# Two float32r parts in place of three bfloat16 parts in the dense products of a two-layer graph network

## The chip, the cores and the metric

The kernel runs on one core of one Trainium2 chip. The metric is the device time of one execution in microseconds (us); the median of the runs shown is 3284.89 us. The engines are TensorE (PE, with its weight loads listed apart as PEld), VectorE (DVE), ScalarE (ACT), GpSimd (POOL) and the queue of SyncE (SP), which issues most of the DMAs.

## The reference, cut to what matters

`x` has 12,500 rows of 256 float32 values, and 200,000 edges lead from row `src` to row `dst`. The edges are sorted by `dst`, and `dst` is far denser at the low rows than at the high ones.

```python
def _sage_conv(x, src, dst, W_l, b_l, W_r):
    msgs = x[src]
    agg = jax.ops.segment_sum(msgs, dst, num_segments=N_NODES)
    deg = jax.ops.segment_sum(jnp.ones((src.shape[0],), x.dtype), dst, num_segments=N_NODES)
    mean = agg / jnp.maximum(deg, 1.0)[:, None]
    return mean @ W_l + b_l + x @ W_r
h = jax.nn.relu(_sage_conv(x, src, dst, W1_l, b1, W1_r))
h = jax.nn.relu(_sage_conv(h, src, dst, W2_l, b2, W2_r))
return h @ W3 + b3
# and around it: layernorm(x + the above)
```

All weights are 256 x 256. The costly part is the sum over the edges, which is made twice: once of rows of `x` and once of rows of `h`.

## The kernel before, in words

Rows are handled in `NB` = 98 blocks of 128, and the 256 columns in `NC` = 2 halves. `layer` (line 602) runs twice, once per layer, and in each layer two ways of summing run side by side.

**Gathered sums.** Edges of the sparse destinations are handled in rounds. A round is four indirect DMAs on POOL (`gathered`, L262), each fetching 128 rows of the table into one of four buffers `got`; then eight short fp32 matmuls on PE (L274) sum neighbouring rows into `part_ps`, ACT copies that to `some` (L284), two fp32 products (L290) spread it over 128 columns, and DVE adds it to a ring of sums (L304). Layer 1 has 269 rounds (1076 indirect DMAs), layer 2 has 235 (940). A buffer `got` can be filled again when the matmuls of the round four earlier are done.

**Dense products.** The densest destinations are handled in groups of `DN` = 256: five in layer 1 (0 to 4), eight in layer 2 (0 to 7). For a group, `count` (L724) makes on PE and DVE a table of how many edges lead from each row to each of the 256 destinations, evicted by ACT (L782) as bfloat16 to one of two buffers `counts`. `product` (L681) then multiplies the rows of the whole table by the counts. Counts are small whole numbers, exact in bfloat16; the float32 rows are made exact as a sum of three bfloat16 parts (`exact`, L656), stored to `x3_d` and `h3_d`. So a block of rows and a group take 3 parts x 2 halves = 6 matmuls of 256 columns (L707), whose stationary operand is a 128 x 128 piece of the rows and whose moving operand is the counts. In layer 2, which needs the same counts of groups 0 to 3 again, layer 1 has saved them to `count_d` (`stored`, L829), and the product of group 4 to 7 from the resident counts runs with that of group 0 to 3 from streamed counts beside it, on the same stationary operand: 12 matmuls a block, alternating between `dense_ps` and `beside_ps`.

Rows come by SP (L693), two blocks a DMA, 384 KB, into `NROWS` = 4 buffers, so eight blocks may be on the way or waiting. A load is made to wait for the gather matmuls that follow the product that read the same buffer four loads earlier (L701), because those matmuls signal anyway.

**Order.** PE and POOL run in the order in which the program emits instructions (`manual_schedule`, L459); the other engines' orders are made by the framework's scheduler. In `layer`, after each gather round the generator `dense` is advanced until its accumulated cost estimate reaches a share of the total that is proportional to the rounds done (`due`, L642), in three thirds with pieces of finished blocks between them. The estimates are constants: `COST_DENSE` 0.7 per block and group, `COST_SPLIT`, `COST_DEGREES`, and `count_cost`. `mixed` interleaves the parts of a stage. In layer 1 a stage is the product of group g-1 beside the count of group g, and the first stage splits `x` beside the count of group 0. Layer 2 has four stages, one per pair of groups, the middle two of them with a count beside.

Finished blocks of 128 destinations go through `first_block` or `last_block` (fp32 matmuls with the weights at L902, L925, L930, L997); `first_block` also stores the block's `h` and its parts.

## Time and profile before

| | |
|---|---|
| median of 3 runs | 3284.89 us (3281.76 to 3287.56) |
| the profiled execution | 3281.46 us, span 3279.7 us |
| mean granted TensorE clock | 0.888 of full speed |
| gather rounds | layer 1 from 11.5 to 1719 us, layer 2 from 1753 to 3234 us |
| DMA | 612.56 MB, mean 187 GB/s |

Busy time of an engine is the sum of its instructions' durations. Matmuls are pipelined, and a matmul's listed duration (282 ns for 256 columns) is longer than the distance from its start to the next one's (0.11 us), so PE's cost is read from distances between starts. "Idle before, releaser" after a group names what ended the waits of that group; "remote" or "another core or an unknown queue" is a semaphore for which the profile finds no sender at that moment. Lines named below are those of the kernel before.

### The profile page before, as it was taken

Reading aid. Unit: us, or ns where it says so; the run is one execution under the profiler, and the core shown is the slowest. Engines: PE = TensorE matmul, PEld = TensorE weight load, DVE = VectorE, ACT = ScalarE, POOL = GpSimd, SP = SyncE. Lnnn points to the kernel's source line nnn. Section 1 sums busy time; section 2 is a strip of 40 time slices with the busy share of each in tenths; the row PEclk is TensorE's granted clock in tenths of the full one; section 3 lists DMA queues with packets and bytes.
Section 4 is the critical chain, followed back from the end, with each engine's and each line's share of the span. In section 5 each row is a group of like instructions: output and inputs, shape, how many; then the busy total and the mean of one; then the engine's idle time right before and its main releaser. Section 6 shows DMA issues by size and latency. Waiting matters only on the chain.

```text
span 3279.7 us, 56146 instructions
## 1 busy us (share of the span) xinstructions
PE 2574.5 (79%) x18946; PEld 1733.1 (53%) x18946; DVE 1566.5 (48%) x5560; ACT 1151.6 (35%) x2331; POOL 1967.7 (60%) x2026
## 2 busy tenths in 40 slices
PE   4565668878878878889865887878889888888876
PEld 2122335545546656656643555556556666666654
DVE  6778675544445555555552122334345444343334
ACT  0423664444444444455441001223233333221122
POOL 6665666666665656666664666565666666556652
PEclk9766679979979989989987899989989999999998
DMA  5565668658658758647644566565556656566642
GB/s 123 164 185 171 179 205 274 209 159 262 209 156 289 225 174 266 221 144 238 222 142 122 181 183 184 176 181 166 177 167 192 184 170 183 164 200 198 204 139 84
DMA packets 375242, 612.56 MB, mean 187 GB/s; under 512 B 72111, under 2 KB 253989, under 8 KB 374949
## 3 DMA queue, kind: packets, MB, share of 16 engines
q1 hardware_dynamic: 273235, 343.33, 34.0%
q0 software_dynamic: 96768, 264.37, 26.7%
q8 instruction: 155, 2.54, 0.3%
q10 hardware_dynamic: 4946, 1.19, 0.2%
q14 instruction: 138, 1.13, 0.1%
HBM read 518.75 MB, written 89.92 MB: 186 GB/s over the span
## 4 chain that ended last, share of the span: by engine, by line
PE 59%; issue 8%; another core or an unknown queue 7%; DVE 5%; ACT 3%; DMA 3%; POOL 0%; ACTq 0%; DVEq 0%; SPq 0%; POOLq 0%
PE dense_ps L707 16%; PE part_ps L274 7%; PE count_ps L776 7%; PE beside_ps L707 6%; PE block_ps L925 6%; PE block_ps L930 5%; PE sum_ps L290 4%; PE block_ps L997 3%; PE block_ps L902 3%; DMA rows<-x_d 2%; ACT counts L782 2%; PE count_ps L780 1%; PE sum_ps L296 1%; PE dense_ps L797 1%
## 5 line engine op out<-in xcount | busy, mean ns | idle before, releaser
L262 POOL DMA_INDIRECT got<-in_x_dram,src_t x1076 | 1067.8, 992 | 649.6 <-issue 258.2
L262 POOL DMA_INDIRECT got<-h_d,src_t x940 | 897.7, 955 | 617.1 <-issue 230.8
L707 PE MATMUL dense_ps<-counts,rows 128*128 128x256 bf16 x5292 | 981.6, 282 | 58.9 <-issue 31.5
L707 PEld LDWEIGHTS <-rows 128*128 128x128 bf16 x7644 | 745.2, 101 | 327.6 <-issue 165.6
L782 ACT CAST counts<-count_ps 128x882 f32 (+3 forms) x688 | 611.3, 888 | 533.1 <-PE count_ps L776 135.6
L707 PE MATMUL beside_ps<-spare,rows 128*128 128x256 bf16 x2352 | 570.3, 282 | 24.2 <-issue 23.2
L776 PE MATMUL count_ps<-pick,low 128*128 128x490 bf16 (+2 forms) x1188 | 378.7, 371 | 145.0 <-ACT counts L782 64.3
L274 PE MATMUL part_ps<-got,one 128*32 128x257 f32 (+1 forms) x4032 | 385.4, 434 | 53.2 <-issue 21.7
L738 DVE TENSOR_SCALAR pick<-steps,key_t 128x686 bf16<-128x686 f16 (+3 forms) x816 | 332.6, 410 | 117.6 <-remote 32.1
L218 DVE TENSOR_TENSOR one<-lo_t,lane_b 128x128 f32<-128x128 bf16 x504 | 144.1, 286 | 470.7 <-remote 150.1
L284 ACT COPY some<-part_ps 128x257 f32<-128x257 f32 (+1 forms) x355 | 132.8, 374 | 643.4 <-remote 293.7
L741 DVE TENSOR_SCALAR low<-lanes,low_t 128x130 bf16<-128x130 f16 x816 | 221.0, 272 | 212.4 <-remote 72.5
L304 DVE TENSOR_TENSOR sums<-sums,sum_ps 128x256 f32 x355 | 145.6, 410 | 250.2 <-remote 110.6
L290 PE MATMUL sum_ps<-two,some 128*128 128x128 f32 x1420 | 241.1, 296 | 13.1 <-issue 8.3
L290 PEld LDWEIGHTS sum_ps<-two,some 128*128 128x128 f32 x1420 | 211.2, 207 | 32.2 <-issue 19.3
L776 PEld LDWEIGHTS <-low 128*128 128x128 bf16 x1188 | 121.1, 103 | 181.9 <-issue 62.7
L936 DVE TENSOR_TENSOR own<-block_ps,biases 128x256 f32<-128x256 f32 x196 | 82.4, 420 | 220.3 <-PE block_ps L930 106.5
L274 PEld LDWEIGHTS part_ps<-got,one 128*32 128x32 f32 x4032 | 89.1, 113 | 184.1 <-issue 161.1
L925 PE MATMUL block_ps<-w1l_sb,sums 128*128 128x256 f32 x352 | 123.5, 483 | 69.7 <-issue 31.5
L933 ACT COPY sums<-zero 128x256 f32<-128x256 f32 x170 | 68.7, 404 | 306.0 <-PE block_ps L930 142.6
L904 ACT COPY own_t<-block_ps 128x256 f32<-128x256 f32 x294 | 109.3, 375 | 183.4 <-remote 65.4
L746 DVE TENSOR_SCALAR aft<-steps,after_t 128x98 bf16<-128x98 f16 x689 | 173.6, 252 | 0.0
(184 smaller groups left out, 2678.7 us busy)
## 6 DMA issues: line engine op xcount, KB each, us to landing
rows<-x_d SPq DMA_DIRECT2D x245, 384.0 KB
rows<-h_d SPq DMA_DIRECT2D x196, 384.0 KB
count_d<-counts SPq DMA_DIRECT2D x28, 896.0 KB
spare<-count_d SPq DMA_DIRECT2D x196, 128.0 KB
x_sb<-in_x_dram SPq DMA_DIRECT2D x194, 128.0 KB
x_d<-split SPq DMA_DIRECT2D x98, 192.0 KB
h_d<-split SPq DMA_DIRECT2D x98, 192.0 KB
got<-in_x_dram,src_t POOLq DMA_INDIRECT x1076
```

The lines of the kernel that those rows point to most:

```text
L262: rows = nc.gpsimd.indirect_dma_start(out=g[:, j, :D], out_offset=None, in_=self.table, in_offset=bass.IndirectOffsetOnAxis(ap=src_t[:, e: ...
L274: strip = nc.tensor.matmul(part_ps[j * W:(j + 1) * W, :width], lhsT=one[:, j], rhs=g[:, j, :width], start=r == 0, stop=r == n - 1)
L290: nc.tensor.matmul(sum_ps[:, c], lhsT=some[:, c * P:(c + 1) * P], rhs=two, start=True, stop=True)
L304: nc.vector.tensor_add(own, own, sum_ps[:, :NC])
L707: nc.tensor.matmul(t[:, c], lhsT=rows[:, b % 2, k, c * P:(c + 1) * P], rhs=d, start=False, stop=b == NB - 1 and k == 2 and c == NC - 1)
L738: nc.vector.tensor_scalar(r[:, :w * NB], steps[:, :w * NB], key_t[g][:, t - lo_g:t - lo_g + 1], None, op0=OP.is_equal)
L741: nc.vector.tensor_scalar(low.rearrange("p (a b) -> p a b", a=5), lanes_5[:, :, :LW // 5], low_t[:, t:t + 1], None, op0=OP.is_equal)
L746: nc.vector.tensor_scalar(aft.rearrange("p (a b) -> p a b", a=7), steps_7[:, :, :NB // 7], after_t[g][:, t - after_from[g]:t - after_from[ ...
L776: nc.tensor.matmul(c[:, a * NB:b * NB], lhsT=s, rhs=r[:, a * NB:b * NB], start=True, stop=alone)
L782: nc.scalar.copy(to[:, :, bass.ds(off_act.at(t), w)], c.rearrange("p (d s) -> p s d", s=NB))
L925: product = nc.tensor.matmul(ps[:, 0], lhsT=agg[:, c], rhs=wl[:, c], start=c == 0, stop=c == NC - 1)
L930: product = nc.tensor.matmul(ps[:, 1], lhsT=own_t[:, c], rhs=wr[:, c], start=c == 0, stop=c == NC - 1)
```

## The change

The rows are split in two float32 parts instead of three bfloat16 parts: the upper part is the float32 value with its low 12 bits cleared by an integer AND, the lower part is the rest. Both have at most 12 significant bits. They are stored as float32 (2048 bytes a row instead of 1536) and multiplied in the type float32r; the counts, which stay bfloat16 in SBUF, are copied to float32 by ACT first (`widened`), into three buffers. Weight loads of float32r are part of the matmul instruction; those of bfloat16 are instructions of their own.

In layer 1 (`product`) a block and a group now take 2 x 2 = 4 matmuls of 256 columns. In layer 2 (`products`) two groups whose counts lie side by side are one moving operand of 512 columns: a block and a pair take 4 matmuls of 512 columns. The pairs are (4,5) resident, then (0,1) and (2,3) streamed while groups 6 and 7 are counted, then (6,7) resident. Rows are loaded one block a DMA (256 KB) into `NROWS` = 6 buffers. A streamed block of a pair's counts is one DMA of 1024 bytes a partition as before. `COST_DENSE` goes from 0.7 to 0.5 and `COST_SPLIT` from 0.8 to 0.7.

Small tables move: the key tables become views of one tensor whose space is used for streamed counts and `w3` in layer 2, offset lists lie in `spare` and in a new `lists`, one bias row and `w3` are loaded between the layers, and `low` has 5 buffers instead of 6. The products' leading matmul with zeros (L689) is left out in layer 2.

```diff
-    x3_d = dram.tile([P, NB, 3, D], BF16, name="x3_d")
-    h3_d = dram.tile([P, NB, 3, D], BF16, name="h3_d")
-    count_d = dram.tile([HG1 - 1, P, NB, DN], BF16, name="count_d")
+    x2_d = dram.tile([P, NB, 2, D], F32, name="x2_d")
+    h2_d = dram.tile([P, NB, 2, D], F32, name="h2_d")
+    SAVED = list(range(HG1 - 1)) + list(range(HG1 + 1, HG - 2))
+    count_d = dram.tile([P, NB, len(SAVED), DN], BF16, name="count_d")
...
-    NROWS = 4
+    NROWS = 6
...
             pieces()
 
-    def exact(t, s, rest):
-
-        def upper(a):
-            return a.bitcast(BF16).rearrange("p (n h) -> p n h", h=2)[:, :, 1]
-
-        leaves = nc.vector.tensor_tensor(rest, t, upper(t), op=OP.subtract)
-        nc.vector.tensor_tensor(s[:, 2], rest, upper(rest), op=OP.subtract)
-        nc.scalar.copy(s[:, 0], upper(t))
-        nc.scalar.copy(s[:, 1], upper(rest))
+    def exact(t, s):
+
+        leaves = nc.vector.tensor_scalar(s[:, 0].bitcast(I32), t.bitcast(I32), -4096, None,
+                                         op0=OP.bitwise_and)
+        nc.vector.tensor_tensor(s[:, 1], t, s[:, 0], op=OP.subtract)
         return leaves
 
     def split_rows(b):
         t = load_rows(x, N, b, "split_sb")
         s = split[:, b % 2]
-        leaves = exact(t, s, work.tile([P, D], F32, name="rest", tag="own"))
+        leaves = exact(t, s)
         if b < 3:
             later(leaves)
-        nc.sync.dma_start(x3_d[:, b], s)
-
-    STREAMS = 4
-    streams = [spare.bitcast(BF16)[:, i * 2 * DN:(i + 1) * 2 * DN].rearrange("p (b d) -> p b d", b=2)
-               for i in range(STREAMS)]
+        nc.sync.dma_start(x2_d[:, b], s)
+
+    STREAMS = 6
+    used_tables = tables[:, :sum(widths[:2 * HG1 + 2])]
+    flat = [(t.bitcast(BF16), n) for t, n in ((spare, 4), (used_tables, STREAMS - 4))]
+    streams = [t[:, i * 2 * DN:(i + 1) * 2 * DN].rearrange("p (g d) -> p g d", g=2)
+               for t, n in flat for i in range(n)]
     n_streamed = 0
 
-    def product(table3, g, c_sb, beside=None):
-
+    def loaded(table2, b, pair=None, ahead=0):
 
         nonlocal n_streamed
-        ps = [dense_pool.tile([P, NC, DN], F32, name="dense_ps")]
-        if beside is not None:
-            ps.append(beside_pool.tile([P, NC, DN], F32, name="beside_ps"))
-        for t in ps:
-            nc.tensor.matmul(t, lhsT=zeros_b, rhs=c_sb[:, :NC, :DN], start=True, stop=False)
+        rows = work.tile([P, 2, D], F32, name="rows", bufs=NROWS)
+        loads = [(nc.sync.dma_start(rows, table2[:, b]), NROWS)]
+        counted = both[:, b, :, :DN]
+        if pair is not None:
+            counted = streams[n_streamed % STREAMS]
+            n_streamed += 1
+            loads.append((nc.sync.dma_start(counted, count_d[:, b, pair:pair + 2]), STREAMS))
+
+        for load, n in loads:
+            n -= ahead
+            if len(used) >= n and used[-n] < len(strips):
+                tc.add_manual_dep(load.ins, strips[used[-n]], LANDED, reason="products done")
+        return rows, counted
+
+    WIDE = 3
+
+    def widened(counted):
+        wide = work.tile([P, 2, DN], F32, name="wide", bufs=WIDE)
+        nc.scalar.copy(wide.bitcast(F32R), counted)
+        return wide
+
+    def product(table2, g, c_sb):
+
+        ps = dense_pool.tile([P, NC, DN], F32, name="dense_ps")
+        nc.tensor.matmul(ps, lhsT=zeros_b, rhs=c_sb[:, :NC, :DN], start=True, stop=False)
+        wide = {}
         for b in range(NB):
-            if b % 2 == 0:
-                rows = work.tile([P, 2, 3, D], BF16, name="rows", bufs=NROWS)
-                loads = [(nc.sync.dma_start(rows, table3[:, b:b + 2]), NROWS)]
-                if beside is not None:
-                    stream = streams[n_streamed % STREAMS]
-                    n_streamed += 1
-                    loads.append((nc.sync.dma_start(stream, count_d[beside, :, b:b + 2]), STREAMS))
-
-                for load, n in loads:
-                    if len(used) >= n and used[-n] < len(strips):
-                        tc.add_manual_dep(load.ins, strips[used[-n]], LANDED, reason="products done")
-            counted = [c_sb[:, b, :DN]] + ([stream[:, b % 2]] if beside is not None else [])
-            n = 0
-            for k in range(3):
+            rows, _ = loaded(table2, b)
+            for u in range(b - b % 2, min(b + 2 * WIDE - 3, NB), 2):
+                if u not in wide:
+                    wide[u] = widened(c_sb[:, u:u + 2, :DN])
+            of = wide[b - b % 2]
+            for k in range(2):
                 for c in range(NC):
-                    for t, d in zip(ps, counted):
-                        nc.tensor.matmul(t[:, c], lhsT=rows[:, b % 2, k, c * P:(c + 1) * P], rhs=d,
-                                         start=False, stop=b == NB - 1 and k == 2 and c == NC - 1)
-                        n += 1
-                        if n == 3 * NC and beside is not None:
-                            yield COST_DENSE
-            if b % 2:
-                used.append(len(strips))
+                    nc.tensor.matmul(ps[:, c], lhsT=rows[:, k, c * P:(c + 1) * P].bitcast(F32R),
+                                     rhs=of[:, b % 2].bitcast(F32R), start=False,
+                                     stop=b == NB - 1 and k == 1 and c == NC - 1)
+            used.append(len(strips))
             yield COST_DENSE
         d_sb = work.tile([P, NC, DN], F32, name="d_sb", bufs=1)
-        nc.scalar.copy(d_sb, ps[0])
+        nc.scalar.copy(d_sb, ps)
         yield g, d_sb
-        if beside is not None:
-            b_sb = split.rearrange("p two k d -> p (two k d)").bitcast(F32)[:, :NC * DN].rearrange(
-                "p (c d) -> p c d", c=NC)
-            nc.scalar.copy(b_sb, ps[1])
-            yield beside, b_sb
+
+    def products(table2, g, pair):
+
+        ps = [pool.tile([P, 2, DN], F32, name=name)
+              for pool, name in ((dense_pool, "dense_ps"), (beside_pool, "beside_ps"))]
+        rows, wide = {}, {}
+        for b in range(NB):
+            for u in range(b, min(b + WIDE, NB)):
+                if u not in wide:
+                    rows[u] = loaded(table2, u, pair, u - b)
+                    wide[u] = widened(rows[u][1])
+            (own, _), of = rows.pop(b), wide.pop(b)
+            for k in range(2):
+                for c in range(NC):
+                    nc.tensor.matmul(ps[c], lhsT=own[:, k, c * P:(c + 1) * P].bitcast(F32R),
+                                     rhs=of.bitcast(F32R), start=b + k == 0,
+                                     stop=b == NB - 1 and k == 1)
+                if k == 0:
+                    yield COST_DENSE
+            used.append(len(strips))
+            yield COST_DENSE
+        d_sb = work.tile([P, NC, DN], F32, name="d_sb", bufs=1)
+        b_sb = split.rearrange("p two k d -> p (two k d)")[:, :NC * DN].rearrange("p (c d) -> p c d", c=NC)
+        for i, t in enumerate((d_sb, b_sb)):
+            for c in range(NC):
+                nc.scalar.copy(t[:, c], ps[c][:, i])
+            yield g + i, t
 
     def count(g, to):
 
...
         nc.vector.reciprocal(rdeg[:, n0:n0 + DN // P], deg)
 
-    COST_DENSE, COST_DEGREES, COST_SPLIT = 0.7, 1.6, 0.8
+    COST_DENSE, COST_DEGREES, COST_SPLIT = 0.5, 1.6, 0.7
 
     def count_cost(t):
         n = 1 if room(t) * NB <= 512 else 2
...
                 p[2] += cost
                 yield cost * scale
 
-    def stored(g, c_sb):
+    def stored(g):
         for b0 in range(0, NB, 14):
-            nc.sync.dma_start(count_d[g, :, b0:b0 + 14], c_sb[:, b0:b0 + 14, :DN])
+            nc.sync.dma_start(count_d[:, b0:b0 + 14, SAVED.index(g)], counts[g % 2][:, b0:b0 + 14, :DN])
             yield 0.5
 
-    def dense(table3, waiting, with_deg, g, c_sb, beside=None):
-        made = []
-        for p in product(table3, g, c_sb, beside):
+    def dense(waiting, made, with_deg=None):
+        ready = []
+        for p in made:
             if isinstance(p, float):
                 yield p
             else:
-                made.append(p)
-        if with_deg:
-            yield from degrees(g, c_sb)
-        for g, d_sb in made:
+                ready.append(p)
+        if with_deg is not None:
+            yield from degrees(with_deg, counts[with_deg % 2])
+        for g, d_sb in ready:
             for j in range(DN // P):
                 waiting.append((g * (DN // P) + j, d_sb[:, :, j * P:(j + 1) * P]))
 
...
     def stages_2(waiting):
 
-        for beside, g in enumerate(range(HG1 - 1, HG)):
-            parts = [(dense(h3_d, waiting, False, g, counts[g % 2], beside), D_2)]
-            if HG1 <= g < HG - 1:
-                parts.append((count(g + 1, counts[(g + 1) % 2]), counting(g + 1)))
-            yield parts
+        def passed(g):
+            pair = SAVED.index(g) if g in SAVED else None
+            return dense(waiting, products(h2_d, g, pair)), D_2
+
+        def next_counts(gs):
+            for g in gs:
+                yield from count(g, counts[g % 2])
+                if g in SAVED:
+                    yield from stored(g)
+
+        yield [passed(HG1 - 1)]
+        before = SAVED[:HG1 - 1:2]
+        for g in range(HG1 + 1, HG, 2):
+            saved = [passed(s) for s in before]
+            yield [(chain.from_iterable(p for p, _ in saved), sum(c for _, c in saved)),
+                   (next_counts((g, g + 1)),
+                    sum(counting(i) + (MOVED if i in SAVED else 0.0) for i in (g, g + 1)))]
+            before = [g]
+        yield [passed(HG - 2)]
 
...
         s = split[:, b % 2]
-        exact(h, s, own)
-        nc.sync.dma_start(h3_d[:, b], s)
+        exact(h, s)
+        nc.sync.dma_start(h2_d[:, b], s)
```

More of the change, by code (lines that the diff above doesn't have):

```diff
@@ L1 @@
 from contextlib import ExitStack
+from itertools import chain
 import concourse.bass as bass
@@ L8 @@
 F32 = mybir.dt.float32
+F32R = mybir.dt.float32r
 F16 = mybir.dt.float16
@@ L140, in by_runs @@
     lo2 = consts.tile([P, len(groups)], F32, name="lo2")
-    place = consts.tile([1, len(groups)], I32, name="place")
     low_t = consts.tile([P, HT], F32, name="low_t")
```

47 lines of the change are left out of this document (30 added, 17 removed).

## The prediction

> **What bounds the kernel now.** I read the page's busy times first, then the chain that ended last, then the costliest groups.
>
> ```profile
> PE 2574.5 (79%) x18946; PEld 1733.1 (53%) x18946; DVE 1566.5 (48%) x5560; ACT 1151.6 (35%) x2331; POOL 1967.7 (60%) x2026
> PE 59%; issue 8%; another core or an unknown queue 7%; DVE 5%; ACT 3%; DMA 3%; POOL 0%; ACTq 0%; DVEq 0%; SPq 0%; POOLq 0%
> L262 POOL DMA_INDIRECT got<-in_x_dram,src_t x1076 | 1067.8, 992 | 649.6 <-issue 258.2
> L707 PE MATMUL dense_ps<-counts,rows 128*128 128x256 bf16 x5292 | 981.6, 282 | 58.9 <-issue 31.5
> L707 PE MATMUL beside_ps<-spare,rows 128*128 128x256 bf16 x2352 | 570.3, 282 | 24.2 <-issue 23.2
> ```
>
> PE is the busiest and holds 59% of the chain, and the products that the change shortens (L707, 7644 matmuls) are its largest part. That alone would promise much. Their real price is in PE's timeline, from start to start:
>
> ```profile
> 2819.82 0.61 PE L290 MATMUL sum_ps<-two,some 128*128 128x128 f32 x4
> 2820.27 0.27 PE L707 MATMUL dense_ps<-counts,rows 128*128 128x256 bf16 x1
> 2820.38 0.27 PE L707 MATMUL beside_ps<-spare,rows 128*128 128x256 bf16 x1
> 2820.49 0.27 PE L707 MATMUL dense_ps<-counts,rows 128*128 128x256 bf16 x1
> ```
>
> A bfloat16 matmul of 256 columns takes 0.109 us. Four fp32 pieces of 128 columns, each with a weight load of its own, take 0.45, so 0.112 each.
>
> But whole stretches tell another story. The columns: us, then busy us and instructions of PE, PEld, DVE, ACT, POOL, then clock, DMA share, GB/s.
>
> ```profile
> 531.00:654.00 123.00, 101.32 (x787) 66.58 (x785) 65.67 (x276) 59.84 (x108) 77.84 (x81) 0.93 0.67 211
> 1817.00:1937.00 120.00, 98.48 (x718) 64.95 (x716) 21.85 (x67) 11.97 (x32) 76.52 (x81) 0.90 0.60 182
> 2955.00:3077.00 122.00, 107.23 (x850) 81.45 (x850) 42.91 (x133) 22.50 (x65) 75.98 (x81) 0.97 0.67 202
> 400.00:1700.00 1300.00, 1069.15 (x8480) 717.55 (x8480) 695.04 (x2679) 627.89 (x1181) 800.87 (x823) 0.89 0.68 212
> 1780.00:3150.00 1370.00, 1155.35 (x8727) 835.38 (x8728) 492.07 (x1587) 334.26 (x711) 833.28 (x873) 0.93 0.60 182
> ```
>
> In the first three, PE issues 718 to 850 matmuls, DVE works 22 to 66 us, ACT 12 to 60, and yet each has 81 gathers in 120 to 123 us: a round of four takes 5.9 to 6.1 us whatever PE does. POOL's timeline shows why:
>
> ```profile
> 2952.68 0.94 POOL L262 DMA_INDIRECT got<-h_d,src_t  x1 [0.30 <-issue]
> 2954.97 0.95 POOL L262 DMA_INDIRECT got<-h_d,src_t  x1 [1.35 <-remote]
> 2956.23 0.95 POOL L262 DMA_INDIRECT got<-h_d,src_t  x1 [0.31 <-issue]
> 2957.48 0.95 POOL L262 DMA_INDIRECT got<-h_d,src_t  x1 [0.30 <-issue]
> 2958.74 0.95 POOL L262 DMA_INDIRECT got<-h_d,src_t  x1 [0.30 <-issue]
> 2961.01 0.95 POOL L262 DMA_INDIRECT got<-h_d,src_t  x1 [1.32 <-PE sum_ps L290]
> ```
>
> Three gathers follow at 1.25 us; the first of a round, which waits for PE's matmuls on its buffer, comes 2.3 us after the one before. 3 x 1.25 + 2.3 = 6.05. The extra 1.04 us is hardly PE's work: PE's completion signals reach the other engines in bursts, and of 2,423 between 60 and 3200 us 678 arrive 1.9 to 2.2 us after the start of the last gather, a time that makes up 4% of that stretch. They come when POOL has just gone idle. Of 503 rounds, 58 start at once (5.0 to 5.2 us), some 270 take 6.0 to 6.4, some 124 over 6.6, and only these last are plainly PE's. Averaged over each layer's stretch (823 and 873 gathers above), a round takes 6.32 and 6.28 us, 0.27 and 0.23 over 6.05.
>
> **The change part by part.**
> *Products, layer 1.* 490 blocks and groups go from 6 x 0.109 to 4 matmuls of 256 columns. No float32r runs before the change, so I bound it: 0.109 (the bfloat16 row) to 0.448 (fp32: two pieces, each 0.112 per 128 columns). I take 0.112, one pass with a weight load like fp32's, because fp32's second piece has nothing to do here and its row shows such a weight load hidden at that spacing. 490 x (0.654 - 0.448) = 101 us.
> *Products, layer 2.* 392 blocks and pairs go from 12 x 0.109 = 1.308 to 4 x 0.224 = 0.896: 162 us. Together 263 us at full clock, 101 / 0.89 + 162 / 0.93 = 288 at the granted one.
> *What of it reaches the end.* PE's work per round falls by about 0.55 and 0.8 us, but the round only down to the 6.05: 206 x 0.27 + 218 x 0.23 = 106 us. If the rounds that start at once rise from 58 to 80, 22 x 1.04 = 23 more. Bounds: nothing, and all 288. PE's instructions for the products fall from 15,288 to 2,058; the issue waits before L707 (31.5 + 23.2 us) may shrink, under the same 6.05.
> *Row loads.* 245 + 196 loads of 384 KB become 490 + 392 of 256 KB: a third more bytes (some 58 MB) and twice the issues at 0.32 us on SP (+140 us there, where x_sb loads and h stores queue behind; SP waits most of the time). Worse, four buffers of two blocks become six of one. A load is released by the gather matmuls after the block six before. Matching each load with its first use, layer 1 gave 6.8 us from issue to use in the median and 3.4 at the 5th percentile, against 2.8 to the last packet; loads went out 2.9 us after their release. Layer 2 gave 17. The page's tile view has layer 1 already short:
>
> ```profile
>   DMA rows<-x_d: 59.1, 42
> ```
>
> In the new PE order 88 rounds of layer 1 hold four or five blocks; the third of them is released only one strip ahead, needed some 3.5 us later and there after 6. Part of that 2.5 falls into PE's present idle of about 1.4 a round; I take 0.4 x 88 = +35 us, bounds -5 and +220.
> *Widening.* ACT gets 245 + 392 copies of 128 x 512; its row `d_sb` (128x512, L716) is 590 ns: 376 us. It loses 392 split copies at 405 ns (L664, L665): 159. The net 217 lie on an engine that is 35% busy (layer 2: 334 of 1370), and its new order puts the copies far ahead of use: cost 0. Each waits for PE's product three before, so `some`, `own_t` and count evictions behind it on ACT may wait, and POOL and PE for them; with streamed counts (196 blocks) ACT also waits for a DMA. Bounds -5 to +45.
> *Splitting.* DVE loses two operations of 414 ns a block and gets an AND and a subtraction; the nearest rows are 272 (L741) and 422 ns (L1008). -15 to +5 us in the first stage, where DVE is 75% busy; I take 0. The larger stores of the parts (98 x 256 KB twice, +12.5 MB) lie beside a stage at 0.62 DMA share, 182 GB/s: 0, or 70 us if that were full.
> *Moved tables, `w3`, a bias, one `low` buffer fewer, 8 zero matmuls gone:* a few us either way, hidden by POOL's rounds; without that cover 8 x 0.2 gained and up to 10 lost between the layers.
> Sum: -106 - 23 + 35 = -94. The profiled execution is 3281.5 (span 3279.7), 3.4 under the median; 3281.5 - 94 + 3 = **3190 us**.
>
> **The rivals.**
> *Half rate (slower, 3480).* The fp32 piece moves 128 columns of 4 bytes in 0.112 us, the bfloat16 matmul 256 columns of 2 bytes in 0.109: the same bytes per time. If float32r is bound by bytes, 256 columns cost 0.224: 490 x (0.896 - 0.654) + 392 x (1.792 - 1.308) = 309 us, 336 at the clock; PE's slack in the rounds hides up to half, +170 to +336. It decides from 0.164 on (1.5 x 0.109). Against it: nothing in the trace shows a one-pass 4-byte operand. The Trainium skill, SBUF — State Buffer, "A bandwidth-pool intuition that's wrong", gives PE's moving operand about 614 GB/s, for 2 bytes a lane at 2.4 GHz; the rows work out at 585 and 601 and agree, which would make this rival the rule. The same skill, FP8 and Floating Point Precision, "TensorE Precision Notes", lists a reduced-precision FP32 that reads 4 bytes and truncates, beside four passes for true FP32; by that it is one pass, and no run so far shows which.
> *Layer 1 starves (slower, 3370).* The late rows cost 88 x 1.7 = 150 in place of 35 and the streamed counts hold ACT for 45, with the 106 gained: 3281 + 89. For it: the 59.1 us above. Against: when POOL waits for PE anyway, signals come sooner.
> *The 6.05 gives way (3060).* With PE far enough ahead half of the rounds start at once, and the mean is 5.6 to 5.7: 206 x 0.62 + 218 x 0.58 = 254, less 35. Against: DVE and ACT live on the same bursts.
> *Weight loads not hidden (3280).* fp32 loads last 207 ns (L290) against 101; at 0.2 for 256 columns layer 1 loses 490 x 0.146 = 72, layer 2 keeps its gain.
>
> **How the numbers follow.** Forecast 0.42 (own range 3120 to 3260), half rate or worse 0.19, starving 0.18, 6.05 gives way 0.14, weight loads 0.05, no effect 0.02. Leaving out the upper part of half rate and the lowest of 3060 gives 3050 to 3470. A measurement tells about 0.2%, 6.6 us. Faster 0.42 + 0.14 + some of the small ones = 0.60, same 0.05, slower 0.35.
>
> **What would show it.** Right: the new matmuls start 0.11 (256) and 0.22 us (512) apart; rounds of layer 2 at 6.0 to 6.1 with PE idle longer; PE busy down far more than the span; the wait for `rows<-x_d` above 59 us. Wrong: spacing of 0.22 and 0.43, rounds under 5.8, layer 1 longer than before, or ACT copies `wide` as the main releaser of PE.

## The result, and the profile after

The changed kernel takes 3368.86 us (median of four runs, 3350.6 to 3378.86) where the kernel before takes 3283.32 in the same comparison: a ratio of 1.0254, 95% interval 1.0208 to 1.030. It is slower by 86 us, where 94 us of gain were forecast. Its profiled execution took 3369.87 us, span 3368.1, mean granted TensorE clock 0.850 (0.888 before).

Page of the changed kernel: busy times, the chain by engine, and the groups of the new products and of the widening copies.

```profile
PE 2452.2 (73%) x14822; PEld 1598.7 (47%) x14822; DVE 1549.2 (46%) x5560; ACT 1386.0 (41%) x2584; POOL 1949.8 (58%) x2026
...
PE 54%; issue 10%; another core or an unknown queue 9%; DMA 9%; DVE 8%; ACT 4%; POOL 2%; SPq 1%; DVEq 0%; ACTq 0%; POOLq 0%
...
L729 PE MATMUL dense_ps<-wide,rows 128*128 128x256 f32 x1960 | 373.5, 324 | 178.4 <-DMA rows<-x_d 150.6
L752 PE MATMUL dense_ps<-wide,rows 128*128 128x512 f32 x784 | 399.4, 509 | 38.2 <-ACT wide L712 18.7
L712 ACT CAST wide<-counts 128x512 fp32r<-128x512 bf16 x441 | 271.2, 620 | 355.6 <-PE dense_ps L729 94.3
```

PE is busy 122 us less and the span is 88 us longer. DMA holds 9% of the chain in place of 3%, and PE stood idle 178 us before the products of layer 1 (L729), 151 of them for their rows.

PE's timeline of the changed kernel in layer 2, start, duration, group:

```profile
2107.35 0.40 PE L752 MATMUL dense_ps<-wide,rows 128*128 128x512 f32 x1
2107.59 0.40 PE L752 MATMUL beside_ps<-wide,rows 128*128 128x512 f32 x1
2107.82 0.61 PE L302 MATMUL sum_ps<-two,some 128*128 128x128 f32 x4
...
2109.61 0.50 PE L752 MATMUL dense_ps<-wide,rows 128*128 128x512 f32 x1
2109.95 0.39 PE L752 MATMUL beside_ps<-wide,rows 128*128 128x512 f32 x1
2110.18 0.40 PE L752 MATMUL dense_ps<-wide,rows 128*128 128x512 f32 x1
```

Within a stretch of products 512 columns take 0.23 to 0.24 us from start to start. At full clock the trace gives a median of 0.118 us for 256 columns and 0.233 for 512: one pass, as forecast (0.112 and 0.224). But the first product of a stretch, which follows a matmul of another kind, holds the next one up for longer, as at 2109.61: 0.223 us (256) and 0.335 (512) in the median, about 0.10 more. In the kernel before the first bfloat16 product of a stretch took 0.110, like the others. The changed kernel has 357 such stretches in layer 1 and 463 in layer 2.

The tile view of the gathers, with the first and last start of each layer at the end of the line, of the kernel before (L262) and the changed kernel (L274):

```profile
L262 POOL DMA_INDIRECT got<-in_x_dram,src_t x1076: 943/949/2259, 11.5 to 1719.3; - x180
L262 POOL DMA_INDIRECT got<-h_d,src_t x940: 942/949/1214, 1753.0 to 3234.1; - x188
L274 POOL DMA_INDIRECT got<-in_x_dram,src_t x1076: 940/946/2390, 11.5 to 1826.5; - x180
L274 POOL DMA_INDIRECT got<-h_d,src_t x940: 940/946/1381, 1858.0 to 3323.2; - x188
```

The changed kernel's tile view of the rows has the idle time until they came (us, times):

```profile
  DMA rows<-x_d: 310.5, 180
```

This view adds up the idle time of all engines that waited, and PE's weight loads (PEld) count as one of them. So a wait of PE stands in it about twice. PE's own waits, for the kernel before and the changed kernel (us, times, longest):

```profile
PE dense_ps L707 <- DMA rows<-x_d: 26.3, 19, 5.7
PE dense_ps L729 <- DMA rows<-x_d: 150.6, 88, 4.8
```

The 59 us of the prediction are 26 of PE and 33 of PEld, the 310 here 151 and 160. The prediction and the expectations go by the sum; the text from here on gives PE's part.

Layer 1's gathers run for 1815 us, 107 more than before (11.5 to 1719.3), layer 2's for 1465, 16 less (1753.0 to 3234.1). So all of the loss lies in layer 1, and layer 2 gave next to nothing back. PE waited 151 us for rows in place of 26, and these 124 us are about the loss.

In windows (us, then busy us and instructions of PE, PEld, DVE, ACT, POOL, then clock, DMA share, GB/s):

```profile
400.00:1700.00 1300.00, 986.94 (x6865) 669.82 (x6863) 635.56 (x2492) 656.16 (x1137) 729.50 (x760) 0.84 0.73 230
```

POOL did 760 gathers in 1300 us of layer 1 where it did 823 before: 6.84 us a round against 6.32. For each gather PE and DVE are, by listed durations, as busy as before (1.30 and 0.84 us; PE at a clock of 0.84 in place of 0.89) and only ACT is busier (0.86 in place of 0.76), on half of its time; what grew is waiting.

PE's timeline in layer 1, with idle time and its releaser in brackets:

```profile
809.92 0.94 PE L729 MATMUL dense_ps<-wide,rows 128*128 128x256 f32 x4 [2.15 <-DMA rows<-x_d]
...
811.80 2.05 PE L729 MATMUL dense_ps<-wide,rows 128*128 128x256 f32 x8 [0.26 <-DMA rows<-x_d]
...
814.75 1.21 PE L729 MATMUL dense_ps<-wide,rows 128*128 128x256 f32 x8
...
821.94 2.25 PE L729 MATMUL dense_ps<-wide,rows 128*128 128x256 f32 x8 [4.12 <-DMA rows<-x_d]
```

Between two strips of gather matmuls (a strip is those of one round) several blocks follow at once, and a later one stands for 2 to 4 us until its rows land. Matched load by load, the buffer is free (its last matmul done) 5.0 us in the median before the next load into it goes out, since that waits for the strip behind the product; from there to the first use it has 5.5 us in the median and 2.8 at the 5th percentile, where a load of the kernel before took 2.8 to its last packet. The trace has 88 rounds of layer 1 with four or five blocks (53 before).

### The profile page after: what moved, and what is told of

Its sections match the earlier page's. It is cut to its first block, busy times and chain, and to the rows that moved or that the text cites. A ratio compares the mean times of both kernels' runs of the same rounds, so it can differ in the third digit from the quotient of the medians.

```text
span 3368.1 us, 48860 instructions
## 1 busy us (share of the span) xinstructions
PE 2452.2 (73%) x14822; PEld 1598.7 (47%) x14822; DVE 1549.2 (46%) x5560; ACT 1386.0 (41%) x2584; POOL 1949.8 (58%) x2026
## 4 chain that ended last, share of the span: by engine, by line
PE 54%; issue 10%; another core or an unknown queue 9%; DMA 9%; DVE 8%; ACT 4%; POOL 2%; SPq 1%; DVEq 0%; ACTq 0%; POOLq 0%
PE part_ps L286 8%; DMA rows<-x_d 8%; PE block_ps L981 7%; PE dense_ps L729 6%; PE count_ps L818 6%; PE block_ps L986 5%; PE dense_ps L752 5%; PE beside_ps L752 5%; PE sum_ps L302 4%; PE block_ps L1053 3%; POOL got L274 2%; PE block_ps L958 2%; ACT counts L824 2%; DVE pick L780 1%
## 5 line engine op out<-in xcount | busy, mean ns | idle before, releaser
L274 POOL DMA_INDIRECT got<-in_x_dram,src_t x1076 | 1050.5, 976 | 774.1 <-PE part_ps L286 364.3
L274 POOL DMA_INDIRECT got<-h_d,src_t x940 | 897.1, 954 | 599.6 <-issue 237.8
L729 PE MATMUL dense_ps<-wide,rows 128*128 128x256 f32 x1960 | 373.5, 324 | 178.4 <-DMA rows<-x_d 150.6
L818 PE MATMUL count_ps<-pick,low 128*128 128x490 bf16 (+2 forms) x1188 | 397.9, 389 | 134.1 <-ACT counts L824 49.8
L752 PE MATMUL dense_ps<-wide,rows 128*128 128x512 f32 x784 | 399.4, 509 | 38.2 <-ACT wide L712 18.7
L712 ACT CAST wide<-counts 128x512 fp32r<-128x512 bf16 x441 | 271.2, 620 | 355.6 <-PE dense_ps L729 94.3
L729 PEld LDWEIGHTS dense_ps<-wide,rows 128*128 128x128 f32 x1960 | 290.0, 208 | 249.7 <-DMA rows<-x_d 159.9
L780 DVE TENSOR_SCALAR pick<-steps,tables 128x686 bf16<-128x686 f16 (+3 forms) x816 | 332.2, 409 | 117.4 <-PE count_ps L818 40.3
L296 ACT COPY some<-part_ps 128x257 f32<-128x257 f32 (+1 forms) x355 | 132.5, 373 | 488.7 <-PE part_ps L286 164.2
L752 PE MATMUL beside_ps<-wide,rows 128*128 128x512 f32 x784 | 330.7, 422 | 0.1
L302 PEld LDWEIGHTS sum_ps<-two,some 128*128 128x128 f32 x1420 | 224.7, 211 | 36.0 <-issue 16.8
L752 PEld LDWEIGHTS dense_ps<-wide,rows 128*128 128x128 f32 x784 | 163.9, 209 | 123.6 <-issue 61.9
L981 PE MATMUL block_ps<-w2l_sb,sums 128*128 128x256 f32 x328 | 115.4, 485 | 107.2 <-issue 26.9
```

What stands on the lines that cost most here:

```text
L274: rows = nc.gpsimd.indirect_dma_start(out=g[:, j, :D], out_offset=None, in_=self.table, in_offset=bass.IndirectOffsetOnAxis(ap=src_t[:, e: ...
L302: nc.tensor.matmul(sum_ps[:, c], lhsT=some[:, c * P:(c + 1) * P], rhs=two, start=True, stop=True)
L712: nc.scalar.copy(wide.bitcast(F32R), counted)
L729: nc.tensor.matmul(ps[:, c], lhsT=rows[:, k, c * P:(c + 1) * P].bitcast(F32R), rhs=of[:, b % 2].bitcast(F32R), start=False, stop=b == NB - ...
L752: nc.tensor.matmul(ps[c], lhsT=own[:, k, c * P:(c + 1) * P].bitcast(F32R), rhs=of.bitcast(F32R), start=b + k == 0, stop=b == NB - 1 and k ...
L780: nc.vector.tensor_scalar(r[:, :w * NB], steps[:, :w * NB], key_t[g][:, t - lo_g:t - lo_g + 1], None, op0=OP.is_equal)
```

## The experiments

**Theory:** layer 1 lost its time to late rows, and layer 2 gained nothing because POOL's gathers and the arrival of PE's signals (the semaphore updates by which it reports that a matmul is done) set its rounds, not PE's work. **Rivals:** PE's work still sets the rounds; the widening copies on ACT; the order by the new constants.

The runs after the first comparison fell on five chips; which chip the first comparison ran on is not on record, and it is counted here as a sixth. The kernel before took 3283 us in the first comparison and 3244 and 3241 on two of the five chips (these are called late), and 2741, 2745 and 2750 on the other three (called prompt); what differs is told at layer 2. Ratios are to the kernel before on the same chip, and expectations that name times near 3300 were written for the first. In the table, the mean rounds are those of rounds 60 to 268 (layer 1) and of all of layer 2, from the starts of POOL's gathers; the wait is PE's own idle time for `rows<-x_d`.

| kernel | chip | ratio (95%) | round, layer 1 | layer 2 | wait for rows |
|---|---|---|---|---|---|
| before | late | 1 | 6.31 | 6.31 | 26 |
| changed | late | 1.025 (1.021 to 1.030) | 6.81 | 6.25 | 151 |
| changed, again | late, second chip | 1.031 (1.029 to 1.034) | 6.77 | 6.24 | 128 |
| changed, third | prompt | 1.044 (1.041 to 1.046) | 5.91 | 5.06 | 161 |

### Late rows

Kernel before, six blocks of lookahead (blocks that may be loaded ahead of their use) in place of eight:

```diff
-    NROWS = 4
+    NROWS = 3
```

> The kernel before with three buffers of two blocks of rows in place of four: six blocks of lookahead, as many as after the change, and nothing else of the change. Theory (the lookahead of the row loads is what layer 1 lost): layer 1's mean round grows from 6.31 toward 6.6 to 6.8 us, the waits of PE for rows<-x_d from 59 us to 150 or more, layer 2 hardly changes, the time rises by 50 to 110 us to 3335 to 3395. Rivals (float32r matmuls with their own weight loads, widening copies, lower clock, the order by new cost constants): none of these is in this kernel, so the time stays within 20 us of 3283.

Measured on a prompt chip: 1.038 (1.036 to 1.040), so 108 us; layer 1 5.83 us a round, layer 2 5.11, 141 us of waits for rows. From its page:

```profile
L707 PE MATMUL dense_ps<-counts,rows 128*128 128x256 bf16 x5292 | 949.0, 277 | 141.2 <-DMA rows<-x_d 141.0
```

Nothing of the change is in it but the shorter lookahead, and it costs nearly what the change costs on a prompt chip (1.044).

The changed kernel with five buffers:

```diff
-    NROWS = 6
+    NROWS = 5
```

> The change with five row buffers in place of six, so five blocks of lookahead. Theory (lookahead): one block less costs again about half of what eight to six cost: layer 1's mean round grows by 0.2 to 0.4 us over the changed kernel's in this call, the time by 40 to 90 us; layer 2, whose loads go out 14 us ahead of use, is unchanged. Rivals (PE, widening, clock, order): within 15 us of the changed kernel.

Measured on the second late chip, beside the changed kernel there: 1.064 (1.059 to 1.070) against 1.031. Layer 1's round went from 6.77 to 7.22, layer 2's stayed at 6.24. In its tile view:

```profile
  DMA rows<-x_d: 476.6, 266
```

Of that, 225 us are PE's, against 128. One block less costs 109 us more, somewhat over what was expected.

The changed kernel with layer 1's loads released by the product that read the buffer, not by the strip after it:

```diff
-            if len(used) >= n and used[-n] < len(strips):
+            if pair is not None and len(used) >= n and used[-n] < len(strips):
```

> The change, with layer 1's row loads no longer made to wait for the gather matmuls that follow the product six blocks earlier; they wait for that product's own last matmul alone, which ends one to two us sooner. Layer 2 is untouched. Theory (late rows): the release comes some 1 to 3 us earlier, PE's waits for rows<-x_d fall from 310 us to under 200, layer 1's mean round from 6.81 to 6.5 to 6.65, the time by 30 to 65 us to 3305 to 3340. Rivals (widening copies, clock, order of work): no change beyond 10 us. A third outcome, slower by 20 us or more, would say that the signals of the extra matmuls cost more than the earlier release brings.

Measured on two prompt chips: 1.0002 (0.998 to 1.002) and 1.0038 (1.002 to 1.006): more than was expected, nearly the whole loss. Layer 1's round is 5.38 and 5.41 us, with 70 and 77 us of waits. A free buffer now waits 0.8 us (median) for its next load, against 4.2 in the changed kernel's own run on a prompt chip, and from issue to use there are 7.4 us in the median, 4.9 at the 5th percentile, against 5.7 and 2.9.

That own run:

> The changed kernel beside the kernel before once more. Two kinds of runs have been seen: with PE's completion signals 0.04 us after a gather matmul's end (the median, and hardly any spread), where the kernel before takes 2741 to 2745 us and layer 2's rounds 5.04; and with signals up to 4 us late, where it takes 3244 to 3283 and layer 2's rounds 6.2 to 6.3. If the signals are prompt: the run with half of layer 2's gathers had layer 1, which it does not touch, at 6.05 us a round, so theory (late rows, whatever the signals) gives layer 1 6.0 to 6.1, layer 2 5.04, 2865 to 2895 us, ratio 1.042 to 1.055. Rival (the loss needs late signals): ratio below 1.02. If the signals are late: 1.025 to 1.032 again.

It came out at 1.044, so the loss needs no late signals. Its tile view of the gathers:

```profile
L274 POOL DMA_INDIRECT got<-in_x_dram,src_t x1076: 940/946/2398, 11.5 to 1604.9; - x180
L274 POOL DMA_INDIRECT got<-h_d,src_t x940: 942/946/1189, 1628.9 to 2816.5; - x188
```

And that of the kernel with released loads, second run:

```profile
L274 POOL DMA_INDIRECT got<-in_x_dram,src_t x1076: 940/946/2372, 11.5 to 1496.5; - x180
L274 POOL DMA_INDIRECT got<-h_d,src_t x940: 942/946/1219, 1520.4 to 2703.5; - x188
```

From the one prompt chip to the other, layer 1's gathers take 108 us less, and layer 2's (1188 and 1183) the same.

The same release in the kernel before, where PE waited only 26 us:

```diff
-                    if len(used) >= n and used[-n] < len(strips):
+                    if beside is not None and len(used) >= n and used[-n] < len(strips):
```

> The kernel before with layer 1's row loads waiting for the last matmul of the product that read the buffer, four loads earlier, and no longer for the gather matmuls behind it. Eight blocks of lookahead stay. Theory (an early release is worth what the lookahead lacks): the kernel before has only 59 us of waits for rows<-x_d, so it gains less than the change did: 0 to 30 us, ratio 0.99 to 1.00. Rival (the released loads help for another reason than late rows, such as fewer signals of the strip matmuls or another order of SP's queue): as much as for the changed kernel, about 100 us, ratio 0.96 to 0.97.

Measured on the second late chip: 0.9984 (0.9966 to 1.0001), with the waits down to 4 us. Where rows are hardly ever late, the release brings hardly anything.

Released loads with a seventh buffer, for whose space one buffer of widened counts is given up:

```diff
-    NROWS = 6
+    NROWS = 7
...
-            if len(used) >= n and used[-n] < len(strips):
+            if pair is not None and len(used) >= n and used[-n] < len(strips):
...
-    WIDE = 3
+    WIDE = 2
```

> The changed kernel with layer 1's loads released by the product itself, seven row buffers in place of six and two buffers of widened counts in place of three (space for one is exchanged for the other), so that ACT widens a pair of blocks only when it is due in layer 1. Theory (lookahead): one more block of lookahead is worth as much again as the early release leaves open, layer 1's waits for rows<-x_d under 60 us, mean round at or below the kernel before's 6.2 to 6.3 (or 5.3), ratio 0.98 to 1.00: a version at least as fast as either kernel. Rival (widening copies bound it, and with two buffers they come late): waits for wide rise above 150 us in layer 1 and the ratio is over 1.01.

Measured on two prompt chips: 0.9938 (0.9915 to 0.9962) and, in a second run, 0.9894 (0.986 to 0.993); layer 1 5.28 and 5.30, waits 55 and 45 us (97 and 83 by the tile view's sum, where under 60 was expected). On these chips it beats both kernels, by 16 and 25 us over the kernel before and by 143 over the changed one beside it. Then on a late chip, the kind on which the change was first measured:

> Released loads, seven row buffers, two widened buffers, for the kind of run with late signals, in which the change was first measured (ratio 1.025 and 1.031, layer 1 at 6.8 us a round). If signals are late: theory (late rows are the whole of layer 1's loss there too) layer 1 6.15 to 6.3 us, layer 2 6.2, ratio 0.985 to 1.00. Rival (part of the loss there is PE's later signals to ACT and SP, which the released loads do not cure): layer 1 above 6.4, ratio above 1.01. If signals are prompt: 0.987 to 0.997, as the two runs before.

Measured: 1.0007 (0.998 to 1.004). Its tile view of the gathers:

```profile
L274 POOL DMA_INDIRECT got<-in_x_dram,src_t x1076: 940/946/2379, 11.5 to 1703.1; - x180
L274 POOL DMA_INDIRECT got<-h_d,src_t x940: 940/946/1254, 1737.9 to 3202.3; - x188
```

And of the rows:

```profile
  DMA rows<-x_d: 44.8, 26
```

PE's part is 27 us. Layer 1's round is 6.27 and its gathers take 1692 us, against 1815 and 1789 of the changed kernel on two such chips. The loss is undone there too; but no gain stands behind it, in either layer. The release alone, with six buffers, ran on prompt chips only.

### The order by the new constants

```diff
-    COST_DENSE, COST_DEGREES, COST_SPLIT = 0.5, 1.6, 0.7
+    COST_DENSE, COST_DEGREES, COST_SPLIT = 0.7, 1.6, 0.8
```

> The change with the planner's constants of the kernel before (0.7 for a block and group, 0.8 for a split, in place of 0.5 and 0.7), so that stages with products get more of the gather rounds and fewer rounds hold four or five blocks. Nothing else. Rival to the theory of the shorter lookahead (the order by the new constants crowds the blocks): layer 1's mean round falls from 6.81 to 6.3 to 6.5 and the time by 60 us or more, to about 3300. Theory (lookahead of six blocks): the crowding is only a part of it, layer 1 stays at 6.6 to 6.85, the time within 40 us of 3369.

Measured on a prompt chip: 1.0151 (1.0134 to 1.0168), layer 1 5.59, waits 136 us. That is 78 us less than the changed kernel on another prompt chip, against "within 40 us" of the theory, so this rival has a part in it: with the old constants 53 rounds hold four or five blocks, with the new ones 88. Six blocks of lookahead are one and a half rounds of four blocks and two of three. PE's waits for rows fell by only 25 us (161 to 136) where layer 1's gathers took 65 us less (1593 to 1528), so what else the old order gives is not shown. With the new constants in place the early release alone brings layer 1 lower still, to 5.38.

### PE's work

The changed kernel with the upper part only:

```diff
-            for k in range(2):
+            for k in range(1):
...
-                for c in range(NC):
+                for c in range(NC if k == 0 else 0):
...
```

> The change with only the upper part of the rows multiplied: half of the float32r matmuls of both layers are left out, and with them the lower 12-bit part of every dense sum; loads, widening copies, counts and gathers stay. That takes 980 x 0.120 = 118 us of PE's work out of layer 1 and 392 x 0.23 = 90 us out of layer 2, 0.44 and 0.41 us a round at the trace's spacings and about 0.5 each at the granted clock. Theory (layer 1 waits for its rows, layer 2 is floored by POOL's cadence of gathers): layer 1's mean round stays within 6.6 to 6.8 us (from 6.81) and layer 2's within 6.1 to 6.25 (from 6.25), the time falls by less than 60 us, to 3310 to 3360. Rival (PE's work sets the rounds): layer 1 falls to about 6.3 and layer 2 to about 5.8, and the time by some 200 us, to about 3170.

Measured on two prompt chips: 1.0455 (1.042 to 1.049) and 1.049 (1.044 to 1.054), no faster than the changed kernel's 1.044. On the second chip layer 1's round was 6.02 us with half the products, and 6.05 in the kernel with fewer gathers in layer 2 (below), whose layer 1 is the changed kernel's. Page of the second run:

```profile
PE 2082.4 (73%) x13058; PEld 1307.0 (46%) x13058; DVE 1540.8 (54%) x5560; ACT 1380.1 (48%) x2584; POOL 1958.1 (68%) x2026
...
L729 PE MATMUL dense_ps<-wide,rows 128*128 128x256 f32 x980 | 261.8, 364 | 229.6 <-DMA rows<-x_d 222.4
```

1764 matmuls are gone (980 of 256 columns, 784 of 512; the expectation counted 392 for these) and nothing is gained: PE waits 222 us for rows, where it waited 164 in the kernel with fewer gathers on the same chip. This run was on prompt chips only.

### The widening copies

```diff
-                if u not in wide:
-                    wide[u] = widened(c_sb[:, u:u + 2, :DN])
-            of = wide[b - b % 2]
+                if not wide:
+                    wide[0] = widened(c_sb[:, u:u + 2, :DN])
+            of = wide[0]
```

> The changed kernel with layer 1's counts widened once a product in place of once for every two blocks: 5 copies in place of 245, so every block of a product is multiplied by the counts of its first two blocks, and the sums of groups 0 to 4 of layer 1 are not the reference's. Loads and matmuls stay. Theory (row loads): layer 1 as in the changed kernel beside it, within 0.1 us a round, the time within 20 us. Rival (ACT's widening copies, 54 us of waits for wide in the first profile of the change, or what queues behind them on ACT): layer 1 0.2 to 0.5 us a round shorter, the time by 40 to 100 us.

Measured beside the changed kernel on the same prompt chip: 1.046 (1.040 to 1.052) against 1.044, layer 1 5.95 us a round against 5.91. From its page:

```profile
L712 ACT CAST wide<-counts 128x512 fp32r<-128x512 bf16 x201 | 124.0, 618 | 137.6 <-PE beside_ps L752 133.4
```

240 copies less, 147 us of ACT's time, and no change: the copies are free in layer 1.

### Layer 2

Layer 1 as before, the change in layer 2 alone (the core of the diff, against the kernel before; `COST_DENSE_3` is layer 1's):

```diff
-    h3_d = dram.tile([P, NB, 3, D], BF16, name="h3_d")
+    h2_d = dram.tile([P, NB, 2, D], F32, name="h2_d")
...
-                rows = work.tile([P, 2, 3, D], BF16, name="rows", bufs=NROWS)
+                rows = rows_pool.tile([P, 2, 3, D], BF16, name="rows", bufs=4)
...
-    COST_DENSE, COST_DEGREES, COST_SPLIT = 0.7, 1.6, 0.8
+    COST_DENSE, COST_DENSE_3, COST_DEGREES, COST_SPLIT = 0.5, 0.7, 1.6, 0.8
```

> The change in layer 2 alone: layer 1 is split in three bfloat16 parts, loaded two blocks a DMA into four buffers and multiplied as before, with the old constants; layer 2 has the two float32r parts, the pairs of 512 columns and the widening copies. Theory (all of the loss is layer 1's row loads; layer 2 is set by POOL): layer 1 as in the kernel before; where POOL's gathers run without a pause in layer 2 the time is within 10 us of the kernel before (ratio 0.997 to 1.004), where rounds take 6.2 it is 10 to 25 us shorter (0.992 to 0.998). Rival (layer 2's products set its rounds): 60 us or more shorter, ratio below 0.98. Rival (widening copies or the larger stores cost something in layer 2): ratio over 1.005.

Measured on the second late chip: 1.0024 (0.9999 to 1.0049): not even the 10 to 25 us. Layer 2's gathers ran 1457 us; in the kernel before with released loads, whose layer 2 is unchanged, they ran 1453 on the same chip.

Two of four gathers a round in layer 2:

```diff
-            for j in range(G):
+            for j in range(2 if self.second else G):
```

> The changed kernel with two of the four gathers of a round in layer 2; the other two buffers keep old rows, so 470 of the 940 gathers of layer 2 are left out of the result. All of PE's, DVE's and ACT's work stays. Theory (POOL's gathers at 1.25 us set layer 2's rounds): the round falls by most of the 2.5 us that two gathers take, until PE's work sets it: from 6.24 (or 5.05) to 4.3 to 5.0 us, layer 2 by 235 x 1.2 to 1.9 = 280 to 450 us where it was 6.24. Rival (PE's work or its signals set them): the round stays over 6.0 where it was 6.24. Layer 1 is untouched at 6.8 (or 5.9).

> The changed kernel with two of layer 2's four gathers a round, for the kind of run with late signals (layer 2 at 6.24 us a round with all four). If signals are late: theory (POOL's gathers, and PE's signals held beside them, set the 6.24) 3.8 to 5.0 us a round. Rival (PE's work or the chain through PE, ACT and DVE) 6.0 to 6.2. If they are prompt: 4.3 again.

On two prompt chips layer 2 took 1007 and 1014 us, 235 rounds of 4.3 us; on a late chip 1015, 4.3 too. The window of layer 2 of the changed kernel on the first chip, columns as above:

```profile
1900.00:2700.00 800.00, 597.42 (x3166) 388.69 (x3166) 270.56 (x897) 317.29 (x609) 498.31 (x523) 0.86 0.66 204
```

And of the kernel with two gathers on a late chip:

```profile
1900.00:2700.00 800.00, 768.28 (x4747) 526.96 (x4740) 428.76 (x1405) 473.69 (x938) 347.29 (x363) 1.00 0.73 230
```

With half of the gathers PE is busy 96% of the time and then sets the pace, at 4.3 us a round. With all of them the window above has 6.1 us a round, of which PE is busy 4.6 (597.42 us in 130.75 rounds, at a clock of 0.86). So 1.5 us or more of each round lay outside PE's work already, and shorter products did not move it.

What lies there differs by chip. The trace lists when PE's completion semaphore rises. In layer 2 of the kernel before in the first comparison the next rise comes about 1.2 us (median; 75th percentile 2.5) after the last matmul of a strip has ended, in the changed kernel about 0.8 (1.8). On the prompt chips it is 0.04, and 0.05 at the 95th percentile, in the changed kernel and in the kernel before with three buffers (the kernel before itself was profiled on the first chip alone). On late chips the trace lists fewer rises than there are signalling matmuls (2497 of 2892 in the kernel before), so these delays may be too long. But an engine that waits shows them as well: where ACT stood idle for a strip, its copy to `some` started 1.9 us (median) after the strip's end in layer 2 of the kernel before, 0.34 in the changed kernel, and 0.07 in its run on a prompt chip.

With two gathers on the late chip the rise comes after 0.04 us in layer 2 as well (90th percentile 0.18), and ACT's copy after 0.07; in layer 1 of the same run, with all four gathers, the rise takes 0.25 (95th percentile 3.4). So on late chips the delay goes when half of POOL's gathers go. Whether the gathers themselves hold the signals back, and how, is not shown; PE also idles less there. POOL's timeline of the changed kernel in layer 2 on the first, late chip:

```profile
2600.62 0.95 POOL L274 DMA_INDIRECT got<-h_d,src_t  x1 [1.38 <-PE beside_ps L752]
...
2609.38 0.95 POOL L274 DMA_INDIRECT got<-h_d,src_t  x1 [0.30 <-issue]
2619.74 0.94 POOL L274 DMA_INDIRECT got<-h_d,src_t  x1 [9.41 <-PE part_ps L286]
```

And in its run on a prompt chip:

```profile
2612.86 0.94 POOL L274 DMA_INDIRECT got<-h_d,src_t  x1 [0.30 <-issue]
2614.11 0.94 POOL L274 DMA_INDIRECT got<-h_d,src_t  x1 [0.30 <-issue]
```

On the prompt chip POOL runs gather after gather at 1.25 us, 5.04 to 5.11 us a round in every kernel with four gathers that was run there; on the late chip it waits, once here for 9.4 us.

## Why the prediction was wrong

- **Products, layers 1 and 2** (101 + 162 us, from 0.112 us per 256 columns): the spacing was right, 0.118 and 0.233 measured, and *half rate* is out. The saving was too large, because the first product of each stretch costs 0.10 us more: an estimate from the trace's starts is 357 x 0.223 + 1603 x 0.118 = 269 us in place of 320 in layer 1 and 463 x 0.335 + 1105 x 0.233 = 413 in place of 513 in layer 2, so about 150 us saved and not 263. *Weight loads not hidden* thus held at the start of a stretch, though not within one. The 2,058 instructions are a slip (490 x 4 + 392 x 4 = 3528), on which nothing rests. The Trainium skill, SBUF — State Buffer, "A bandwidth-pool intuition that's wrong", gives PE's moving operand about 614 GB/s for bfloat16. Here 128 x 256 x 4 bytes in 0.118 us are 1111 GB/s, so that figure is no limit for float32r. The Trainium skill, FP8 and Floating Point Precision, "TensorE Precision Notes", lists a reduced-precision FP32 beside four passes for true FP32, which the prediction read as one pass; the spacing agrees.
- **What of it reaches the end** (-106 and -23): wrong, and the larger error. The step took all time above 6.05 us a round for PE's work, and the rounds over 6.6 us as "plainly PE's". Half of the products left out brought nothing on two prompt chips. In layer 2 the rounds over 6.6 became more, from 70 to 85, though PE had less to do in each; those that start at once rose as forecast (43 to 66) and the mean went from 6.31 only to 6.25. The two-gather run has PE at 4.3 us; the 6.3 were POOL's gathers and late signals. With the late rows cured the kernel on a late chip ends at 1.0007: about 0 in place of -129.
- **Row loads** (+35): the mechanism was right, down to the 88 rounds, and the size wrong. On late chips the changed kernel stands 2.5 to 3.1% over the kernel before, with the rows cured 0.1%: 80 to 100 us, inside the bounds of -5 to +220. I took 0.4 us for each of 88 rounds; in fact rounds 60 to 268 grew by 0.51 each in the mean. The idle of 1.4 us a round that was to absorb part of the wait (1.1 by the window from 400 to 1700 us) did not: PE's waits grew by 124 us and layer 1's gathers by 107.
- **Widening** at 0: right, shown for layer 1. **Splitting** and stores were not tried by themselves; the first product starts at 488.7 us in place of 478.4.
- **Sum:** about 0 + 86 in place of -129 + 35.
- **Rival "Layer 1 starves", 3370:** the time to 1 us, but by another sum. Its 150 for the rows was too much, its 45 for the copies was 0, and its gain of 106 was not there.
- **"The 6.05 gives way":** it does, to 5.04 to 5.11, on the prompt chips, in the kernel before with three buffers as well; it is no effect of the change.

What stays open: why the chips differ, and whether the gathers themselves hold PE's signals back; whether the release alone cures a late chip too; how much of the 80 to 100 us the crowded rounds hold on a late chip, since the old constants ran on a prompt one; what the old constants give beside shorter waits; and in the version with seven buffers, what the seventh gives by itself (on one chip, 0.9938 against 1.0038 with six and three widened buffers).

## What to carry to other kernels

Before an engine's saved work is counted, take work away from the engine that paces the round (two gathers of four) or from the engine itself (half the products): if the time doesn't follow the second, shorter instructions there are worth nothing. When a change makes loads smaller, count their lookahead in time, blocks times time per block from the release to the use, not in buffers; shorter products crowd together and shrink it again. A view that adds up the waits of several engines can count one wait twice: read the waiting engine alone. Where a load's release is tied to a later signal to save signals, the tie is only free while the lookahead covers it.

## What the runs showed of the hardware

- The same program took 2741 to 2750 us on three chips and 3241 to 3283 in three other comparisons. The changed kernel's gathers last the same on both kinds (median 946 ns); the difference goes with the delay of PE's signals, 0.04 us at the median in either layer against 0.2 to 1.2 (kernel before about 0.7 in layer 1 and 1.2 in layer 2, changed kernel 0.2 and 0.8).
- The delay was down to 0.04 us (median) in layer 2 on a late chip when POOL had half of its gathers there.
- A float32r matmul of 256 columns starts 0.118 us after the one before it in a stretch, and one of 512 columns 0.233; after the first of a stretch it is 0.223 and 0.335. A bfloat16 matmul of 256 columns has 0.109, and 0.110 after the first.
- The granted clock was lower where PE idled more: 0.888 before (PE busy 79%), 0.850 after (73%), 0.86 in the window of layer 2 with PE busy 75%, and 1.00 in the same window with PE busy 96% (on two late chips). The Trainium skill, TensorE: Matmul & The Clock Gate, Part 1, says that the default state is throttled and that activity releases the throttle; the rows agree.
